# Attention's source alphas by staged one-hot products in pass 2, in place of gathers on POOL

## The chip, the cores and the metric

One core of a Trainium2 chip runs the whole program in one launch. The metric is the device time in microseconds (us): before the change 4203.94 us, the median of 10 runs that lie between 4200.74 and 4207.65 us.

A core has a matrix engine (PE; its weight loads are listed apart as PEld), VectorE (DVE), ScalarE (ACT), GpSimd (POOL), a queue engine (SP) that here only issues transfers, and 16 DMA engines. SBUF is the working memory with 128 lanes, PSUM holds what PE puts out, and DRAM holds the tables.

## The reference, cut to what matters

There are 12500 nodes of 256 features and 200000 edges (src, dst), sorted by dst. The first part is a graph convolution block with a residual; the second is an attention block that uses only the first n = 12500 edges.

```python
def gcn_conv(x, W, b):            # src, dst with one self loop per node added
    h = x @ W
    norm = dinv[src] * dinv[dst]
    return segment_sum(h[src] * norm[:, None], dst, n) + b

h = relu(layernorm(x))
h = h @ W_pre + b_pre
h = relu(gcn_conv(h, W1, b1)); h = relu(gcn_conv(h, W2, b2))
x = x + (h @ W_post + b_post)

h = relu(layernorm(x))
xt = (h @ weight).reshape(n, 4, 64)
alpha_l = sum(xt[src] * attn_l, -1)      # one number for each edge and head
alpha_r = sum(xt[dst] * attn_r, -1)
alpha = softmax(leaky_relu(alpha_l + alpha_r, 0.01), over the 4 heads)
tmp = sum over heads of alpha[:n, h] * xt[dst[:n], h]
out = x + the 64 columns of tmp, repeated 4 times
```

Row i of the attention's result belongs to edge i. Its dst is one of the first nodes, since edges are sorted by dst; its src is any node. So alpha_l of a row may need any node of the graph, the last one too.

## The kernel before, in words

**Tiles.** A tile is 128 edges, a chunk J = 14 tiles (1792 edges). There are 112 chunks, and NT = 98 windows of 128 nodes. The attention's 12500 edges are the first AC = 7 chunks, 98 tiles. Each attention chunk touches at most 128 nodes as dst, all within the first XW = 9 windows.

**The two passes.** `convolve` runs once for each convolution. For each tile POOL issues an indirect DMA that gathers 128 rows of the table by src (L1179, into fgot, four chunk buffers), and PE multiplies them by a one-hot of the edges' dst (L1187, into facc). VectorE builds a chunk's one-hots in one instruction (fhot, L1073; its node numbers are kept in PSUM as iota_p). When a chunk is done, ACT copies its sums (L1103), PE transposes them (L1038), and VectorE adds them into a sliding buffer (L1120). When the last edge of a window has been added, the window's own steps run: they are closures in a list, each with a number of tiles after which it is due, so that the instructions of a window's end stand between the products of later tiles. The instructions of each engine are in the order in which this list emits them.

**A window's end in pass 2** (`finish2`): the matrix W2 (d, L1269), bias and relu, W_post (f, L1285), the sum with the residual and its storing as kept_x (g), layernorm statistics, relu (h), transposes (i), a copy (k, ht, L1315), and the product with wg (q, L1324), which has 256 columns of xt, 4 of alpha_r and 4 of alpha_l. Step r (L1332) lets ACT copy the result and issue transfers: the alpha_l columns to the DRAM tables table_l and table_e, and for the first XW windows xt and alpha_r to table_r. The last LW = 3 windows don't write to table_e. Step names such as "fpx" in the list say which PSUM tile a step fills; a step that fills one waits in the list until it is read.

**Rows by dst.** For chunk c of the attention, `own_rows(c)` (L1374) is one gather on POOL of 128 consecutive rows of table_r; chunk 0 in window FROM = 40, the other six after pass 2. `turn_hots` (L1369) builds a one-hot of the edges' dst on VectorE. The rows of a tile are then one product of the two; those of the first 14 tiles are made during windows 40 to 53 (L1350, kept in `early`), the others in the last stage.

**The last stage, called the tail below.** The 98 tiles are handled in 15 groups: 13 of seven tiles, one of four and one of three. For each group:

- `keep` (L1418): SP loads kept_x. `ends_of` (L1446, L1448): PE makes the seven tiles' rows (256 columns of xt[dst] and 4 of alpha_r) through two PSUM buffers (fends), and ACT copies them to fxg in SBUF.
- `mix`: POOL gathers alpha_l by src, one indirect DMA for a tile (fal, L1456): 84 of table_l and, for the first 14 tiles, of table_e. What table_e lacks is added for these from three one-hots (hot_l, built at the start of pass 2, L1390) by `missing` (L1427).
- VectorE makes the softmax (L1460 to L1472, the exponential on ACT), scales the four heads (near and far, L1479), adds them (some L1482, more L1484, fmix L1486) and adds kept_x (fres, L1488). SP stores the group (L1494, L1497).

`keep` and `ends_of` of a group stand two groups ahead of its `mix`. Only SP and ACT issue direct transfers here; the gathers go through POOL's queue.

## Time and profile before

The profiled execution took 4204.65 us, of which the span from the first to the last instruction is 4202.8 us. The mean granted clock of PE is 0.797 of full speed.

| stretch (us from the start) | length | PE | DVE | ACT | POOL | granted clock | GB/s |
|---|---|---|---|---|---|---|---|
| start, 0 to 127 | 127.0 | 72.1 | 89.0 | 68.7 | 41.1 | 0.72 | 221 |
| pass 1, 127 to 2083 | 1956.0 | 1538.7 | 367.0 | 114.1 | 1477.7 | 0.78 | 121 |
| pass 2, 2083 to 4057 | 1974.0 | 1417.5 | 534.0 | 241.4 | 1486.9 | 0.83 | 130 |
| tail, 4057 to 4202.8 | 145.8 | 79.8 | 108.4 | 35.0 | 94.9 | 0.68 | 210 |

The engines' columns are busy us. A busy share under 100% doesn't mean that an engine has slack: POOL's time between two gathers is the issue of the next one, which the profile doesn't count as busy. Lines of the groups read "line, engine, operation, out<-in, count | busy us, mean ns of one | idle us before, and what ended it".

### The profile page before, as it was taken

Reading aid. Unit: us, or ns where it says so; the run is one execution under the profiler, and the core shown is the slowest. Engines: PE = TensorE matmul, PEld = TensorE weight load, DVE = VectorE, ACT = ScalarE, POOL = GpSimd, SP = SyncE. Lnnn points to the kernel's source line nnn. Section 1 sums busy time; section 2 is a strip of 40 time slices with the busy share of each in tenths; the row PEclk is TensorE's granted clock in tenths of the full one; section 3 lists DMA queues with packets and bytes.
Section 4 is the critical chain, followed back from the end, with each engine's and each line's share of the span. In section 5 each row is a group of like instructions: output and inputs, shape, how many; then the busy total and the mean of one; then the engine's idle time right before and its main releaser. Section 6 shows DMA issues by size and latency. Waiting matters only on the chain. (4 is left out here: it accounts for less than half of the span.)

```text
span 4202.8 us, 31693 instructions
## 1 busy us (share of the span) xinstructions
PE 3108.1 (74%) x10423; PEld 1960.2 (47%) x10423; DVE 1098.5 (26%) x2260; ACT 459.3 (11%) x1155; POOL 3100.5 (74%) x3346
## 2 busy tenths in 40 slices
PE   6487787787878788877667777777777777777774
PEld 5254444444444444444355545554455545455552
DVE  7321111111111111111132222222222222222238
ACT  5100000000000000000001111111111111111122
POOL 3677777777777777777777777777777777777766
PEclk7678878777777877788888888888888888877886
DMA  6544444444444444444445545554454445444556
GB/s 214 160 121 119 118 122 122 118 119 122 120 121 117 122 121 121 119 121 121 129 137 140 130 128 128 132 128 127 128 132 127 128 127 132 128 127 127 132 162 202
DMA packets 326197, 551.36 MB, mean 131 GB/s; under 512 B 96041, under 2 KB 224520, under 8 KB 326024
## 3 DMA queue, kind: packets, MB, share of 16 engines
q0 software_dynamic: 153520, 414.27, 37.3%
q1 hardware_dynamic: 126966, 118.80, 9.4%
q10 hardware_dynamic: 45538, 16.17, 1.5%
q8 instruction: 86, 1.41, 0.1%
q14 instruction: 87, 0.71, 0.1%
HBM read 495.73 MB, written 53.19 MB: 131 GB/s over the span
## 5 line engine op out<-in xcount | busy, mean ns | idle before, releaser
L1179 POOL DMA_INDIRECT fgot<-ftable,fsrc_t x3112 | 2944.7, 946 | 957.1 <-issue 898.0
L1187 PE MATMUL facc<-fgot,fhot 128*128 128x257 f32 (+1 forms) x6252 | 2368.4, 498 | 912.2 <-DMA fgot<-ftable,fsrc_t 870.5
L1187 PEld LDWEIGHTS facc<-fgot,fhot 128*128 128x128 f32 x6252 | 1265.8, 233 | 1856.6 <-DMA fgot<-ftable,fsrc_t 1410.7
L1120 DVE TENSOR_TENSOR buf<-buf,fturn 128x256 f32 x224 | 94.5, 422 | 1730.4 <-PE fturn L1038 1364.3
L1073 DVE TENSOR_TENSOR fhot<-iota_p,to_t 128x1792 f32<-128x1792 f32 x224 | 448.6, 2004 | 4.4 <-PE fpt L1094 4.4
L1276 DVE SCALAR_TENSOR_TENSOR fy<-rb,fb2c,fpz 128x128 f32<-128x128 f32 x194 | 58.8, 345 | 736.1 <-PE fpz L1269 735.1
L1103 ACT ACTIVATE fsums<-facc 128x257 f32<-128x257 f32 (+1 forms) x224 | 86.2, 385 | 1248.3 <-PE facc L1187 1242.4
L1290 DVE SCALAR_TENSOR_TENSOR fx<-fpo,fdinv,fxb 128x256 f32<-128x256 f32 x97 | 46.9, 484 | 477.5 <-PE fpo L1285 477.5
L1220 PE MATMUL fpo<-wf,buf 128*128 128x256 f32 x388 | 158.0, 552 | 0.4 <-DVE buf L1120 0.4
L1225 ACT ACTIVATE fo<-fpo,fdinv 128x256 f32<-128x256 f32 x97 | 46.0, 474 | 784.6 <-PE fpo L1221 784.6
L1220 PEld LDWEIGHTS fpo<-wf,buf 128*128 128x128 f32 x388 | 114.5, 296 | 29.6 <-DVE buf L1120 0.7
L1269 PE MATMUL fpz<-buf,fwb 128*128 128x128 f32 x776 | 123.8, 312 | 0.0
L1269 PEld LDWEIGHTS fpz<-buf,fwb 128*128 128x128 f32 x776 | 121.4, 235 | 2.3 <-DVE fy L1276 0.3
L1038 PE MATMUL fturn<-fident,self 128*128 128x128 f32 x396 | 84.0, 297 | 40.0 <-DMA self<-ftable 36.3
L1285 PE MATMUL fpo<-fwo,fz 128*128 128x256 f32 x388 | 112.3, 414 | 0.3 <-ACT fz L1279 0.3
L1456 POOL DMA_INDIRECT fal<-table_l,fsrc_t x84 | 81.2, 967 | 25.6 <-issue 23.2
L1038 PE MATMUL fturn<-fident,fsums 128*128 128x128 f32 x448 | 96.1, 300 | 0.5 <-ACT fsums L1103 0.5
L1446 PE MATMUL fends<-rows,hot_t 128*128 128x260 f32 x168 | 67.1, 566 | 35.9 <-ACT fxg L1448 35.4
L1315 ACT ACTIVATE ht<-fpt 128x256 f32<-128x256 f32 x97 | 37.2, 384 | 473.2 <-PE fpt L1311 473.2
L1038 PEld LDWEIGHTS fturn<-fident,fsums 128*128 128x128 f32 x448 | 70.5, 158 | 31.4 <-issue 8.4
L1221 PE MATMUL fpo<-bb,fins 2*128 2x256 f32 x194 | 85.1, 524 | 0.0
L1149 DVE COPY buf<-fturn 128x256 f32<-128x256 f32 x190 | 78.1, 411 | 0.0
(225 smaller groups left out, 1533.7 us busy)
## 6 DMA issues: line engine op xcount, KB each, us to landing
fgot<-ftable,fsrc_t POOLq DMA_INDIRECT x3112, 2.8
ftable<-fxt SPq DMA_DIRECT2D x14, 910.0 KB
self<-ftable SPq DMA_DIRECT2D x99, 128.0 KB
self<-ftable SPq DMA_DIRECT2D x97, 130.0 KB
ftable<-fo ACTq DMA_DIRECT2D x98, 128.0 KB
kept_x<-fx SPq DMA_DIRECT2D x98, 128.0 KB
fxb<-in_x_dram SPq DMA_DIRECT2D x97, 128.0 KB
fxt<-in_x_dram SPq DMA_DIRECT2D x13, 896.0 KB
```

The lines of the kernel that those rows point to most:

```text
L1038: nc.tensor.transpose(v["pt"][:, i * KC + k, :], rows[:, k * P:(k + 1) * P], ident)
L1073: nc.vector.tensor_tensor(h, iota_p[:, None, :].to_broadcast([P, n, P]), to[:, :, None].to_broadcast([P, n, P]), ALU.is_equal)
L1103: nc.scalar.activation(sb, acc, AF.Copy)
L1120: nc.vector.tensor_add(b, b, v["pt"][:, :KC, :])
L1149: nc.vector.tensor_copy(nxt[:, :, new], v["pt"][:, KC:, :])
L1179: nc.gpsimd.indirect_dma_start(out=got, out_offset=None, in_=table[:(NT - TW) * P, :] if some else table[:], in_offset=bass.IndirectOffset ...
L1187: nc.tensor.matmul(acc, hots[c][:, j, :], got[:, :width], start=(j == 0), stop=(j == nj[c] - 1 and not some))
L1220: nc.tensor.matmul(po, buf[:, k, :P], wf[:, k, :], start=(k == 0), stop=False)
L1221: nc.tensor.matmul(po, fs, bb, start=False, stop=True)
L1269: nc.tensor.matmul(pz[:, m, :], wb[:, k, m * P:(m + 1) * P], buf[:, k, :P], start=(k == 0), stop=(k == KC - 1))
L1285: nc.tensor.matmul(po, v["z"][:, m, :], wo[:, m, :], start=(m == 0), stop=(m == KC - 1))
L1456: nc.gpsimd.indirect_dma_start(out=al[:, i, :], out_offset=None, in_=(table_l if c else table_e)[:], in_offset=bass.IndirectOffsetOnAxis(a ...
```

## The change

The alpha_l of an edge is no longer fetched by a gather. A src is split into its low 7 bits and its window (src >> 7). The alpha_l columns of all windows stay in SBUF (`l_all`, 128 lanes by 98 windows by 4 heads). For a tile of edges, one product of a one-hot of the low bits with the columns of several windows gives, for each edge, the value at its lane in each of these windows; a mask "window equals src >> 7", a product and a sum pick the one that counts (`add_picked`), which is added to `al`.

This runs in five stages over windows 0 to 18, 18 to 36, 36 to 54, 54 to 72 and 72 to 84, each as soon as its windows are there. A part (`product` and `taken`) covers seven tiles, that is 70 parts of seven products of 72 columns (48 in the last stage); parts are appended to the steps of pass 2's windows, one to a window and two from window 73 on. Seven further parts first make alpha_r of all tiles, with 14 products of 4 columns each, and put it into `al`. Windows 84 to 97 (56 columns) follow in the tail (`late_al`). The one-hots of low bits are built one at a time, in two buffers, during pass 2 (`next_hot`: 44 in all), from a row that SP broadcasts to all lanes (`load_lo`).

`own_rows` becomes seven direct loads on SP in window 11, each with a register load of its first row. The writes to table_l and table_e go, and so do hot_l, `lates` and `missing`.

The tail is ordered anew: the softmax is made for a batch of four groups, heads 0 and 1 are scaled by ACT in pieces of 64 columns (`shared`), heads 2 and 3 by VectorE as before, fmix is in SBUF, and the sum with kept_x is made by POOL. Rows by dst are made up to six groups ahead (`fxg` has six buffers).

The other `own_rows`, `turn_late`, `keep` and out transfers keep their content and change place. The diff, cut:

```diff
-    table_l = dram.tile([NT * P, H], F32, name="table_l")
-    LW = 3
-    table_e = dram.tile([NT * P, H], F32, name="table_e")
+    lo_rows = dram.tile([NT, P], BF16, name="lo_rows")
+    STAGES = [(0, 18), (18, 36), (36, 54), (54, 72), (72, 84)]
+    LATE = STAGES[-1][1]
+    NL_W = NT - LATE
...
+    def split_sources(work):
...
+        lo = work.tile([NT, P], BF16, name="lo_b", bufs=1)
+        nc.vector.tensor_copy(lo, r)
+        nc.sync.dma_start(lo_rows, lo)
+        h = work.tile([P, NT], I32, name="hi_i", bufs=1)
+        nc.vector.tensor_scalar(h, src_t[:, :AC, :].rearrange("p c j -> p (c j)"),
+                                P.bit_length() - 1, None, op0=ALU.arith_shift_right)
+        nc.vector.tensor_copy(hi_t, h)
...
+    l_all = ap.tile([P, NT, H], F32, name="l_all", bufs=1)
+    al = ap.tile([P, NT, H], F32, name="al_all", bufs=1)
...
         def r():
...
-            nc.scalar.activation(xa[:, d0:], v["px"], AF.Copy)
-            nc.scalar.dma_start(table_l[w * P:(w + 1) * P, :], xa[:, DR:])
-            if w < NT - LW:
-                nc.scalar.dma_start(table_e[w * P:(w + 1) * P, :], xa[:, DR:])
             if w < XW:
-                nc.scalar.dma_start(table_r[w * P:(w + 1) * P, :], xa[:, :DR])
+                xa = work.tile([P, DR], F32, name="fxa", bufs=1)
+                nc.scalar.activation(xa, v["px"][:, :DR], AF.Copy)
+                nc.scalar.dma_start(table_r[w * P:(w + 1) * P, :], xa)
+            nc.scalar.activation(l_all[:, w, :], v["px"][:, DR - d0:], AF.Copy)
...
+        o = steps[-1][0] + 2
+        if w == XW + 2:
+            steps.append((o, own_rows, None))
+            steps.append((o + 2, next_hot, None))
+        for _ in range(0 if w < XW + 4 else 1 if w < STAGES[-2][1] + 1 else 2):
+            if todo and todo[0][0] <= w:
+                _, product, taken = todo.pop(0)
+                steps += [(o, lambda f=product: f(psum), "fpx"), (o + 2, lambda f=taken: f(work), None)]
+                o += 4
         return steps
...
-    def own_rows(c):
-        nc.gpsimd.indirect_dma_start(
-            out=rows[c], out_offset=None, in_=table_r[:],
-            in_offset=bass.IndirectOffsetOnAxis(ap=row_i[:, c:c + 1], axis=0))
+    def own_rows():
+        for c in range(AC):
+            at = nc.values_load(base_i[0:1, c:c + 1], engines=(mybir.EngineType.SP,), min_val=0,
+                                max_val=(XW - 1) * P,
+                                skip_runtime_bounds_check_because="clamped on the chip")
+            nc.sync.dma_start(rows[c], table_r[bass.ds(at, P), :])
...
+    def load_lo(pool, c, bufs):
+        lo = pool.tile([P, CE], BF16, name="lo_all", bufs=bufs)
+        nc.sync.dma_start(lo, lo_rows[c * J:(c + 1) * J, :].rearrange("t p -> (t p)")
+                          .partition_broadcast(P))
+        return lo
+    def next_hot():
+        if not coming:
+            return
+        key, row = coming.pop(0)
+        hot = hot_of[key] = ap.tile([P, CE], F32, name="hot_s", bufs=2)
+        s, c = key
+        nc.vector.scalar_tensor_tensor(hot, row[0], base_b[:, c:c + 1] if s == "ends" else 0.0,
+                                       in_banks["lane"].to_broadcast([P, CE]),
+                                       op0=ALU.subtract, op1=ALU.is_equal)
+        if coming:
+            coming[0][1].append(coming[0][1].pop()())
+    def stage_parts(work):
+        def ends_part(c):
+            z = {}
+            def product(psum):
+                z["p"] = psum.tile([P, 512], F32, name="fpx", bufs=1)[:, :J * H]
+                z["p"] = z["p"].rearrange("p (t h) -> p t h", h=H)
+                for j in range(J):
+                    nc.tensor.matmul(z["p"][:, j, :], hot_of["ends", c][:, j * P:(j + 1) * P],
+                                     rows[c][:, D:], start=True, stop=True)
+            def taken(work):
+                nc.scalar.activation(al[:, c * J:(c + 1) * J, :], z["p"], AF.Copy)
+                next_hot()
+            return XW + 4, product, taken
+        def al_part(s, c, b):
+            w0, w1 = STAGES[s]
+            nw, t0, z = w1 - w0, c * J + b * G, {}
+            def product(psum):
+                z["p"] = psum.tile([P, 512], F32, name="fpx", bufs=1)[:, :G * nw * H]
+                z["p"] = z["p"].rearrange("p (t w h) -> p t w h", t=G, h=H)
+                for i in range(G):
+                    j = b * G + i
+                    nc.tensor.matmul(z["p"][:, i, :, :], hot_of[s, c][:, j * P:(j + 1) * P],
+                                     l_all[:, w0:w1, :], start=True, stop=True)
+            def taken(work):
+                add_picked(work, z["p"], w0, w1, t0, in_banks["iota"])
+                if b == 0 or (s, c) == (len(STAGES) - 1, AC - 1):
+                    next_hot()
+            return w1 + 1, product, taken
+        todo.extend(ends_part(c) for c in range(AC))
+        todo.extend(al_part(s, c, b) for s in range(len(STAGES)) for c in range(AC)
+                    for b in range(J // G))
+        for s in ["ends"] + list(range(len(STAGES))) + ["late"]:
+            for c in range(AC if s != "late" else 2):
+                coming.append(((s, c), [(lambda c=c: load_ends(work, c, 1)) if s == "ends" else
+                                        (lambda c=c: load_lo(work, c, 1))]))
...
+    def add_picked(pool, z, w0, w1, t0, iota):
+        n, nw = z.shape[1], w1 - w0
+        mask = pool.tile([P, G, max(b - a for a, b in STAGES)], F32, name="fmask", bufs=1)
+        mask = mask[:, :n, :nw]
+        nc.vector.tensor_tensor(mask, iota[:, None, w0:w1].to_broadcast([P, n, nw]),
+                                hi_t[:, t0:t0 + n, None].to_broadcast([P, n, nw]), ALU.is_equal)
+        nc.vector.tensor_tensor(z, z, mask[:, :, :, None].to_broadcast([P, n, nw, H]), ALU.mult)
+        some = pool.tile([P, G, H], F32, name="fsome", bufs=1)[:, :n, :]
+        nc.vector.tensor_reduce(some, z.rearrange("p t w h -> p t h w"), AX.X, ALU.add)
+        o = al[:, t0:t0 + n, :]
+        nc.vector.tensor_add(o, o, some)
...
+        stage_parts(work)
...
+        def turn_lo(c):
+            if c in los:
+                hot_a[c] = mp.tile([P, CE], F32, name="hot_a", bufs=2)
+                nc.vector.tensor_scalar(hot_a[c], los[c], lane, None, op0=ALU.is_equal)
...
-        def missing(g):
...
+            xa = ends[g] = mp.tile([P, G, D], F32, name="fxg", bufs=6)
             for i in range(n):
                 c, j = divmod(t0 + i, J)
...
-                px = psum.tile([P, DR], F32, name="fends", bufs=2)
-                nc.tensor.matmul(px, hot_t[c][:, j * P:(j + 1) * P], rows[c], start=True,
+                px = psum.tile([P, D], F32, name="fends", bufs=2)
+                nc.tensor.matmul(px, hot_t[c][:, j * P:(j + 1) * P], rows[c][:, :D], start=True,
                                  stop=True)
                 nc.scalar.activation(xa[:, i, :], px, AF.Copy)
...
-            al = mp.tile([P, G, H], F32, name="fal", bufs=4)
+        def late_al(g):
+            t0, n = groups[g]
+            z = psum.tile([P, G * NL_W * H], F32, name="flate", bufs=2)[:, :n * NL_W * H]
+            z = z.rearrange("p (t w h) -> p t w h", t=n, h=H)
             for i in range(n):
                 c, j = divmod(t0 + i, J)
-                nc.gpsimd.indirect_dma_start(
-                    out=al[:, i, :], out_offset=None, in_=(table_l if c else table_e)[:],
-                    in_offset=bass.IndirectOffsetOnAxis(ap=src_t[:, c, j:j + 1], axis=0))
-            s = mp.tile([P, G, H], F32, name="fs")[:, :n, :]
-            nc.vector.tensor_add(s, al[:, :n, :], xa[:, :, D:])
-            if t0 < J:
-                nc.vector.tensor_add(s, s, missing(g))
+                nc.tensor.matmul(z[:, i, :, :], hot_a[c][:, j * P:(j + 1) * P],
+                                 l_all[:, LATE:, :], start=True, stop=True)
+            add_picked(mp, z, LATE, NT, t0, iota_w)
...
+        def softmax(b):
+            t0 = groups[batches[b][0]][0]
+            n = min(4 * G, NT - t0)
+            s = al[:, t0:t0 + n, :]
...
+            nc.vector.tensor_mul(s, s, m[:, :, None].to_broadcast([P, n, H]))
+        h2 = H // 2
+        def shared(g):
+            (t0, n), xa = groups[g], ends[g]
+            near = shares[g] = mp.tile([P, h2, G, C], F32, name="near", bufs=2)
+            for i in range(n):
+                for h in range(h2):
+                    nc.scalar.activation(near[:, h, i, :], xa[:, i, h * C:(h + 1) * C], AF.Copy,
+                                         scale=al[:, t0 + i, h:h + 1])
+        def mix(g):
+            (t0, n), xa, xr = groups[g], ends.pop(g)[:, :groups[g][1], :], kept.pop(g)
+            near, xr = shares.pop(g)[:, :, :n, :], xr[:, :n, :]
+            share = psum.tile([P, G, h2], F32, name="share", bufs=1)[:, :n, :]
+            nc.vector.tensor_copy(share, al[:, t0:t0 + n, h2:])
             far = psum.tile([P, h2, 512], F32, name="far", bufs=1)
...
-            for v, o in ((near, 0), (far, h2)):
-                nc.vector.tensor_mul(v.rearrange("p h g c -> p g h c"), xh[:, :, o:o + h2, :],
-                                     share[:, :, o:o + h2, None].to_broadcast([P, n, h2, C]))
+            nc.vector.tensor_mul(far.rearrange("p h g c -> p g h c"),
+                                 xa[:, :, h2 * C:].rearrange("p g (h c) -> p g h c", h=h2),
+                                 share[:, :, :, None].to_broadcast([P, n, h2, C]))
             some = mp.tile([P, G, C], F32, name="some")[:, :n, :]
...
-            mixed = psum.tile([P, G, C], F32, name="fmix", bufs=1)[:, :n, :]
+            mixed = mp.tile([P, G, C], F32, name="fmix")[:, :n, :]
             nc.vector.tensor_add(mixed, some, more)
             res = mp.tile([P, G, D], F32, name="fres", bufs=2)[:, :n, :]
-            nc.vector.tensor_add(res.rearrange("p g (h c) -> p g h c", h=H),
-                                 xr.rearrange("p g (h c) -> p g h c", h=H),
-                                 mixed[:, :, None, :].to_broadcast([P, n, H, C]))
+            nc.gpsimd.tensor_tensor(res.rearrange("p g (h c) -> p g h c", h=H),
+                                    xr.rearrange("p g (h c) -> p g h c", h=H),
+                                    mixed[:, :, None, :].to_broadcast([P, n, H, C]), ALU.add)
...
+        NG1 = len(groups)
+        for g in range(3):
+            keep(g)
+        for g in range(4):
+            late_al(g)
+            ends_of(g)
+        softmax(0)
+        for c in range(2, 4):
+            turn_late(c)
+            turn_lo(c)
+        for g in range(4, 8):
+            ends_of(g)
+        shared(0)
+        for g in range(NG1):
+            if g + 1 < NG1:
+                shared(g + 1) if g + 1 not in [b[0] for b in batches] else None
+            mix(g)
+            if g + 3 < NG1:
+                keep(g + 3)
+            if g + 4 < NG1:
+                late_al(g + 4)
+                if g % 2:
+                    turn_lo(g // 2 + 4)
+            for b in range(1, len(batches)):
+                if g + 1 == batches[b][0]:
+                    softmax(b)
+                    shared(g + 1)
+            if g >= 2 and g + 6 < NG1:
+                if g % 2 == 0:
+                    turn_late(g // 2 + 3)
+                ends_of(g + 6)
```

## The prediction

> **What bounds the kernel now.** I read the page first (busy shares, groups), then a table of stretches over the end of pass 2 and the tail, then the chain, and last the lines of single instructions.
>
> ```profile
> PE 3108.1 (74%) x10423; PEld 1960.2 (47%) x10423; DVE 1098.5 (26%) x2260; ACT 459.3 (11%) x1155; POOL 3100.5 (74%) x3346
> L1179 POOL DMA_INDIRECT fgot<-ftable,fsrc_t x3112 | 2944.7, 946 | 957.1 <-issue 898.0
> L1456 POOL DMA_INDIRECT fal<-table_l,fsrc_t x84 | 81.2, 967 | 25.6 <-issue 23.2
> ```
>
> A gather costs POOL 0.946 us and 0.30 us of issue, 1.25 us in all. 3112 of them are 3890 us: POOL sets the pace of both passes. In the tail 98 more (84 from table_l, 14 from table_e) are 122.5 us.
>
> The stretches (length, busy us of PE, PEld, DVE, ACT, POOL, clock, DMA share, GB/s):
>
> ```profile
> 2200.00:4000.00 1800.00, 1306.71 (x4915) 923.03 (x4914) 476.32 (x1016) 222.87 (x592) 1361.36 (x1441) 0.82 0.50 129
> 4100.00:4120.00 20.00, 11.90 (x33) 6.85 (x32) 18.37 (x33) 5.89 (x18) 15.13 (x17) 0.82 0.72 234
> 4120.00:4140.00 20.00, 13.99 (x36) 8.45 (x36) 18.35 (x33) 7.24 (x22) 15.43 (x16) 0.69 0.76 234
> 4140.00:4160.00 20.00, 12.69 (x36) 7.12 (x34) 18.61 (x31) 6.27 (x19) 15.12 (x17) 0.80 0.73 230
> ```
>
> The chain (start, us, what) goes through the tail's gathers, but these rows show a second bound beside them: VectorE is busy 18.4 of 20 us. A group of seven tiles takes it 7.8 us, against 8.75 us of gathers. So taking the gathers away frees at most the difference; the rest comes only if VectorE's and the other queues' work per group shrinks.
>
> ```profile
> 4057.16 1.37 DMA table_l<-fxl
> 4058.53 0.93 POOL fal L1456
> ...
> 4158.34 2.27 DMA fal<-table_l,fsrc_t
> ...
> 4194.86 0.95 DVE fres L1488
> ```
>
> The first alpha of the last window leaves ACT at 4057.98, the last sum ends at 4195.81, and 7.0 us later its output has landed: the tail is 145 us of the span.
>
> **Pass 2, part by part.** POOL loses one own-row gather in window 40: -1.25 us. The other six (4041 to 4048) lay beside the last windows: 0.
> PE gets 98 + 490 products of 4 and 72 columns, each two instructions. Rows: 42 instructions with 4 columns took 5.85 and 6.70 us, 776 with 128 columns 123.8 us, so 0.14 to 0.16 us each, 0.3 per product, 176 us in all. Cover: PE's wait for gathers, 493.6 us in 2200 to 4000, 5.3 us a window. One part (7 products, 2.1 us) fits; two a window (4.2 us, windows 73 to 79 and 85 to 91) just fit, and four chunk buffers let POOL run 56 gathers, 70 us, ahead. So 0; without the cover up to 176.
> VectorE gets 44 one-hots (2.02 us, the fhot row's size) and 70 picks: mask 0.22, product and reduction of 504 values 0.65 each (448 take 0.62), sum 0.18, 1.7 us. 208 us on an engine 26% busy: 0.
> SP gets seven register loads with row loads in window 11 and 44 broadcast loads, 23 MB over some 1550 us (15 GB/s onto 129); behind them wait only the next window's rows, asked for a window (19 us) ahead. ACT loses two DMA issues a window. Both 0.
> One price remains on POOL: the short sum of a pick has both operands in SBUF. At 4143.53 such a one-hot from SBUF to SBUF (1.20 us) stretched the gather under it from 0.94 to 1.44 us, 40% of its length. 70 sums of 0.18 us then cost 0 to 12.6 us, by that row 5; three hot_l of the pass start go, -1.4. Pass 2 together: +2 (bounds -3 to +10).
>
> **The tail.** The order on the queues decides, which I walk through from 4056.7 (4057.98 less 1.25).
> To the first result. PE: late products of groups 0 to 3 (28 at 0.27 us, between the two rows above) and end rows of groups 2 to 7, 42 tiles. A tile cost 0.61 us (4.25 for seven, 4153.94) to 0.84 (5.88, 4058.03, clock 0.5); PE now runs without a gap, and in 2135 to 2156 such a run was at clock 1.00, so 0.62: 26 us. With masks and waits PE is through at 4093.4. ACT copies these end rows in order, and only behind them stands the scaling of group 0, 14 pieces. A piece of 64 by rows: copies of 4 and 256 columns take 0.174 and 0.384, so 0.22; a per-lane scale adds 0.09 (fo 0.474 against ht 0.384); neighbours overlap by 0.1: 0.2 to 0.25, I take 0.225, 3.2 us. VectorE adds its last 1.9 us: group 0 ends at 4098.9. Before, group 0 was out at 4081.5: 17.4 us behind, with VectorE idle from 4081.
> Groups 1 to 3. VectorE per group: share, far, some, more, mix 3.2 us (rows 1.09, 0.62, 0.62, 0.63), pick 0.2 + 0.57 + 0.57 + 0.2 for 392 values, a one-hot of 1.2 in two of three. That is 5.6. But the output sum now runs on POOL, right where VectorE's pick begins, and this trace shows what two such instructions do to each other:
>
> ```profile
> 10.19 2.80 DVE L634 TENSOR_TENSOR near_f<-fdst_r,low 112x1792 f32<-112x1792 int32 x1
> ...
> 9.98 1.13 POOL L622 TENSOR_SCALAR_AFFINE_SELECT sel<-sel 32x1024 f32<-32x1024 f32 x1
> 11.18 2.77 POOL L624 TENSOR_SCALAR_AFFINE_SELECT sel<-sel 32x1024 f32<-32x1024 f32 x1
> ```
>
> POOL's first select ends at 11.11; VectorE's two-operand sum, issued at 10.19, takes 0.9 us more than its 1.9 and ends when 11.1 + 1.9 is over; the second select, alone 1.08, waits for that until 12.99. One stands still while the other works. So the pick's last sum waits for POOL's output sum. POOL's price for 1792 values from two operands is in no row: below it lies the one-operand select's rate (1.08 us for 1024), 1.9 us; above it that rate for each operand, 3.8. The short two-operand rows (14 values 0.209, 42 values 0.254, 1.6 ns a value) give 3.1; I take 3.4, as short rows hide a rate. The group is then mix 3.2 + mask 0.2 + POOL 3.4 + sum 0.2 + 0.8 of one-hots = 7.8, as before: group 3 ends at 4122.2.
> Groups 4 to 7. A softmax batch and the scaling behind it open the stretch (13.6 us for group 4); after it PE's seven end rows 4.4, late products 1.9 and ACT's 3.2 in between make 9.1 to 9.6 a group; POOL hides under them. Group 7: 4163.0. Group 8, after a softmax, 4175.4. Groups 9 to 11, without end rows, 7.0 each: 4196.3. Last softmax (its subtraction waits for POOL) and scaling, 10.1; the two short groups 2.2 and 1.7: 4210.3. POOL, one sum and one landed output behind, ends at 4216.3; 7.0 us as before: 4223.3. By DMA's sums the stretch would not bind (some 32 MB at the 335 GB/s seen at 4064 to 4078 is 96 us).
>
> **Two rules of the skill that speak against the change.** The Trainium skill, GPSIMD Engine Reference, section 3.1, has POOL's two-operand add about twice as slow as VectorE's, 4497 ns for 2048 values. By that an estimate of the output sum is 3.95 us and the end 4.7 us later than with 3.4. The Trainium skill, SBUF — State Buffer, section "SBUF: two separate sides", calls the port pair of both an exclusive lock for the whole instruction; the two rows at 10 us agree. Were it not so, the sum would end at 4206.8.
>
> **Sum.** Span 4223.3 + 2 in pass 2 = 4225; around it lie 1.85 us (4204.65 less 4202.8): 4227. The profiled run is 0.7 us above the median of 4203.94, so 4226.
>
> **Rivals.** (a) The two engines do not shut each other out here, or POOL's sum costs the lower bound. Groups 0 to 3 and 9 to 11 then take 5.6 and 4.3 us, no waits: end 4206.8 and 4210.8, with pass 2 and the frame 4210 to 4214; with PE at its full clock throughout 4 us less. For it: most tail operations of VectorE have one operand in PSUM. Against it: mask, sum and softmax have not.
> (b) Faster: the queues overlap so well that VectorE's own work alone sets the pace. 13 us to the first softmax, 74 us of its work (15 x 3.15, 11 x 1.55, softmax 6, one-hots 6), some 12 of waits and 10 to the landing: 4166, 37 us faster. It decides once ACT scales group 0 near 4080, not 4093; half of that effect, with (a) and full clock, is 4193. Against it: ACT's order puts 28 copies before the scaling, and PE cannot deliver 42 tiles under 0.45 us each (the dense run's pace).
> (c) Slower still: pass 2 stops hiding the products, since VectorE's picks and PE wait on each other through one PSUM tile (2 us for each of 70 parts, 140 us in all) and POOL runs out of its 70 us of lead: 4230 to 4300. Against it: 493 us of slack.
> (d) PE stays at clock 0.5 to 0.7 in the tail as now: end rows 0.84, end 4234.6 to 4238, the upper end of the forecast: 4242.
>
> **Chances.** Within 0.2% (8.4 us, about what a measurement of this kernel can tell) lies 4195.5 to 4212.3. Forecast with (d), 4213 to 4246: 0.57; (a), mostly inside the band: 0.20; (b), from 4166 to about 4198: 0.18; (c): 0.05. That gives slower 0.62, same 0.18, faster 0.20. The range 4193 to 4246 leaves out most of (b) and (c); the forecast's own is 4213 to 4246.
>
> **What would show it.** Right: the 40 slices unchanged up to the last; POOL's gathers still 1.25 us apart in pass 2; VectorE idle from about 4081 to 4097 behind ACT; POOL's output sum 3 to 4 us, and VectorE's short sum in the pick as long as what is left of it. Wrong: the first output sum before 4090 (b), short sums of 0.2 us throughout (a), or waits of the gathers on PE (c).

## The result and the profile after

The changed kernel takes 4235.73 us (median of 8 runs, 4230.76 to 4240.42), against 4206.22 us (28 runs) of the kernel before beside it: a ratio of 1.0073, with a 95% interval of 1.0064 to 1.0082. It is about 30 us slower; 4226 was forecast.

The profiled execution has a span of 4228.8 us, 5 us under the median once the 1.8 us around it are added. The lines of its page that answer to those shown before (engine sums, then groups):

```profile
PE 3228.2 (76%) x11711; PEld 2103.1 (50%) x11711; DVE 1288.1 (30%) x2552; ACT 507.8 (12%) x1356; POOL 3051.3 (72%) x3256
...
L1196 POOL DMA_INDIRECT fgot<-ftable,fsrc_t x3112 | 2942.7, 946 | 956.9 <-issue 899.8
...
L1448 PEld LDWEIGHTS fpx<-l_all,hot_s 128*128 128x128 f32 x980 | 147.3, 228 | 5.4
L1588 POOL TENSOR_TENSOR fres<-fxr,fmix 128x1792 f32<-128x1792 f32 (+2 forms) x15 | 55.7, 3714 | 129.4 <-DVE fmask L1472 61.5
L1448 PE MATMUL fpx<-l_all,hot_s 128*128 128x72 f32 (+1 forms) x980 | 143.1, 308 | 0.0
```

The gathers of the passes are what they were: 946 ns each, 900 us of issue. The 98 gathers of the tail are gone, and in their place POOL makes 15 output sums. The 490 stage products, two instructions each, keep PE busy for 143 us of pass 2, 0.29 us a product (0.3 was forecast), and POOL doesn't notice: from the first gather of pass 2 to the last one's end it takes 1957.3 us before and 1954.1 us after (1954.3 to 1960.0 in later profiles of kernels with the new alphas).

So the loss lies in the tail. Its cleanest measure is the stretch from the last copy of alpha_l (the last instruction of pass 2 on ACT) to the end of the span, since the passes end up to 13 us apart in two profiles of the changed kernel. Before, it is 144.8 us (4058.0 to 4202.8); after, 179.6 (4049.2 to 4228.8).

The table of stretches of the tail after (length, busy us of PE, PEld, DVE, ACT, POOL, clock, DMA share, GB/s):

```profile
4073.50:4091.50 18.00, 17.71 (x60) 9.83 (x61) 4.39 (x5) 10.55 (x28) 0.00 (x0) 0.91 0.41 153
4098.00:4118.00 20.00, 3.45 (x15) 3.33 (x16) 19.17 (x24) 7.20 (x30) 10.79 (x3) 0.50 0.70 217
4130.00:4170.00 40.00, 27.14 (x112) 19.79 (x112) 22.61 (x41) 22.99 (x82) 15.88 (x4) 0.77 0.55 169
```

Three regimes follow each other. From 4073.5 PE and ACT make end rows and VectorE idles. From 4098 VectorE is the one that is busy (19.17 of 20 us), but a good part of that is waiting. From 4130 no engine is busy for more than 70%: they wait for each other. ACT's rows (start, us, what, idle before) show the end of the first regime:

```profile
4090.17 0.84 ACT L1533 ACTIVATE fxg<-fends 128x256 f32<-128x256 f32 x2 [0.33 <-PE fends L1531]
4091.34 0.39 ACT L1533 ACTIVATE fxg<-fends 128x256 f32<-128x256 f32 x1 [0.33 <-PE fends L1531]
4091.62 6.78 ACT L1568 ACTIVATE near<-fxe,al_all 128x64 f32<-128x64 f32 x28
```

The 28th copy of end rows of groups 4 to 7 ends at 4091.7, and only then are heads 0 and 1 of groups 0 and 1 scaled. VectorE's rows, with its wait for that, and POOL's beside them:

```profile
4094.85 0.62 DVE L1582 TENSOR_TENSOR some<-near,far 128x448 f32<-128x448 f32 x1 [16.93 <-ACT near L1568]
...
4098.15 2.77 DVE L1478 TENSOR_TENSOR al_all<-al_all,fsome 128x28 f32<-128x28 f32 x1
...
4105.55 2.59 DVE L1478 TENSOR_TENSOR al_all<-al_all,fsome 128x28 f32<-128x28 f32 x1
...
4125.86 0.19 DVE L1478 TENSOR_TENSOR al_all<-al_all,fsome 128x28 f32<-128x28 f32 x1
...
4199.62 3.70 DVE L1554 TENSOR_TENSOR al_all<-al_all,fm 128x56 f32<-128x56 f32 x1
```

```profile
4096.90 3.98 POOL L1588 TENSOR_TENSOR fres<-fxr,fmix 128x1792 f32<-128x1792 f32 x1 [61.53 <-DVE fmask L1472]
4104.14 3.96 POOL L1588 TENSOR_TENSOR fres<-fxr,fmix 128x1792 f32<-128x1792 f32 x1 [3.26 <-DVE fmix L1586]
...
4218.63 1.80 POOL L1588 TENSOR_TENSOR fres<-fxr,fmix 128x768 f32<-128x768 f32 x1 [2.69 <-DMA out_dram<-fres]
```

The same short sum of 28 values takes 0.19 us at 4125.86, when POOL is at rest, and 2.77 and 2.59 us beside POOL's sums: 4098.15 + 2.77 is 4100.92, and POOL's sum ends at 4100.88; 4105.55 + 2.59 is 4108.14 against 4108.10. The last line of POOL's rows is the end of the tail: its last sum waits another 2.69 us for one of two fres buffers, whose output has to land.

### The profile page after: what moved, and what is told of

It is laid out like the page before. It is cut to its first block, busy times and chain, and to the rows that moved or that the text cites. A ratio compares the mean times of both kernels' runs of the same rounds, so it can differ in the third digit from the quotient of the medians.

```text
span 4228.8 us, 34731 instructions
## 1 busy us (share of the span) xinstructions
PE 3228.2 (76%) x11711; PEld 2103.1 (50%) x11711; DVE 1288.1 (30%) x2552; ACT 507.8 (12%) x1356; POOL 3051.3 (72%) x3256
## 5 line engine op out<-in xcount | busy, mean ns | idle before, releaser
L1204 PE MATMUL facc<-fgot,fhot 128*128 128x257 f32 (+1 forms) x6252 | 2328.9, 488 | 797.9 <-DMA fgot<-ftable,fsrc_t 763.5
L1204 PEld LDWEIGHTS facc<-fgot,fhot 128*128 128x128 f32 x6252 | 1225.9, 227 | 1721.9 <-DMA fgot<-ftable,fsrc_t 1381.2
L1448 PEld LDWEIGHTS fpx<-l_all,hot_s 128*128 128x128 f32 x980 | 147.3, 228 | 5.4
L1588 POOL TENSOR_TENSOR fres<-fxr,fmix 128x1792 f32<-128x1792 f32 (+2 forms) x15 | 55.7, 3714 | 129.4 <-DVE fmask L1472 61.5
L1448 PE MATMUL fpx<-l_all,hot_s 128*128 128x72 f32 (+1 forms) x980 | 143.1, 308 | 0.0
L1237 PEld LDWEIGHTS fpo<-wf,buf 128*128 128x128 f32 x388 | 113.5, 293 | 29.2 <-DVE buf L1137 0.7
L1531 PE MATMUL fends<-rows,hot_t 128*128 128x256 f32 x168 | 59.9, 504 | 43.3 <-DVE share L1575 22.9
L1474 DVE TENSOR_TENSOR fpx<-fpx,fmask 128x504 f32<-128x504 f32 (+1 forms) x70 | 46.0, 657 | 142.4 <-PE fpx L1448 141.2
```

The lines of the kernel that those rows point to most:

```text
L1204: nc.tensor.matmul(acc, hots[c][:, j, :], got[:, :width], start=(j == 0), stop=(j == nj[c] - 1 and not some))
L1237: nc.tensor.matmul(po, buf[:, k, :P], wf[:, k, :], start=(k == 0), stop=False)
L1448: nc.tensor.matmul(z["p"][:, i, :, :], hot_of[s, c][:, j * P:(j + 1) * P], l_all[:, w0:w1, :], start=True, stop=True)
L1531: nc.tensor.matmul(px, hot_t[c][:, j * P:(j + 1) * P], rows[c][:, :D], start=True, stop=True)
```

## The experiments

Theory: the tail is slow because (1) ACT's order holds up the first group, (2) VectorE's instructions with two operands in SBUF stand still while POOL's sum runs, and (3) what the new alphas add to the tail (late products and picks) is more than the removed gathers freed. Rivals: PE's end rows set the pace whatever the order; the stretched sums are contention with DMA; taking the gathers away wins and only the new tail loses.

The first four runs went to a chip on which the gathers of both passes had to wait, for a reason that the traces don't show, and the kernel before took 4952.03 us. Whole times can't resolve the tail there, so those runs are read by the stretch, one profile for each kernel. (Their whole times were 1.0029, 1.0004, 0.9978 and 0.9966 of the kernel before, in the order below; only the last interval, 0.9934 to 0.9998, leaves out 1.) That the stretch doesn't depend on the chip is shown by two kernels that ran on both: 158.9 and 159.4 us, 159.2 and 158.5 us. Differences under 1 us are not read.

**The sum back on VectorE.**

```diff
+            bank = psum.tile([P, 512], F32, name="share", bufs=1)
...
-            mixed = mp.tile([P, G, C], F32, name="fmix")[:, :n, :]
+            mixed = bank[:, 64:].rearrange("p (g c) -> p g c", c=C)[:, :n, :]
...
-            nc.gpsimd.tensor_tensor(res.rearrange("p g (h c) -> p g h c", h=H),
-                                    xr.rearrange("p g (h c) -> p g h c", h=H),
-                                    mixed[:, :, None, :].to_broadcast([P, n, H, C]), ALU.add)
+            nc.vector.tensor_add(res.rearrange("p g (h c) -> p g h c", h=H),
+                                 xr.rearrange("p g (h c) -> p g h c", h=H),
+                                 mixed[:, :, None, :].to_broadcast([P, n, H, C]))
```

> The sum with kept_x goes back from POOL to VectorE (2.02 us a group there, fmix in PSUM again); all else as changed. Theory, queue order and mutual exclusion: the pick's last sum falls from 2.6 to 3.1 us to 0.2, so VectorE's groups stay near 7 us, but the last softmax is 3.5 us shorter and POOL's late sums at the end go: span about 4219 (4215 to 4222), against 4228.8. Rival, PE and the late products set the pace of the tail and POOL's sum is hidden: no gain, 4226 to 4232. Rival, the stretched sums come from DMA traffic and not from POOL: they stay over 1 us, and the span is longer, 4235 to 4250.

The stretch is 172.0 us, 7.6 less, as the theory had it (7 to 14). All pick sums are back at 0.17 to 0.19 us with the same transfers running, so POOL and not DMA stretched them. VectorE now spends 2.02 us a group on the sum itself, which takes back a part of what is won.

**One operand in SBUF.**

```diff
+        bank = psum.tile([P, 512], F32, name="share", bufs=1)
+        iota_b = bank[:, 256:256 + NT]
+        in_banks["some"] = bank[:, 16:16 + G * H]
...
-            add_picked(mp, z, LATE, NT, t0, iota_w)
+            add_picked(mp, z, LATE, NT, t0, iota_b)
...
-            nc.vector.scalar_tensor_tensor(s, s, SLOPE, s, op0=ALU.mult, op1=ALU.max)
-            m = mp.tile([P, 4 * G], F32, name="fm")[:, :n]
+            lo = bank[:, 128:128 + n * H].rearrange("p (t h) -> p t h", h=H)
+            nc.vector.tensor_scalar(lo, s, SLOPE, None, op0=ALU.mult)
+            nc.vector.tensor_tensor(s, s, lo, ALU.max)
+            m = bank[:, 64:64 + n]
```

> POOL keeps the output sum; in the tail every instruction of VectorE that had two operands in SBUF (mask, the pick's last sum, the softmax's leaky relu, subtraction and product) gets one of them in PSUM. Theory, mutual exclusion of POOL and two-operand instructions: POOL's sums stay at 3.97 us, the pick's last sum takes 0.2 us beside them, groups 1 to 3 follow each other in 4.9 to 5.9 us instead of 7.2 to 8.4, groups 4 to 7 stay at PE's pace, and the span is 4211 to 4217. Rival, plain contention for SBUF: the short sums stay over 1 us or POOL's sums grow, and the span is within 5 us of 4228.8.

The stretch is 169.3 us, 10.3 less; 12 to 18 was expected. VectorE's and POOL's rows in this kernel:

```profile
4847.52 0.18 DVE L1481 TENSOR_TENSOR al_all<-al_all,share 128x28 f32<-128x28 f32 x1
...
4852.46 0.18 DVE L1481 TENSOR_TENSOR al_all<-al_all,share 128x28 f32<-128x28 f32 x1
4852.56 3.40 DVE L1508 TENSOR_SCALAR hot_a<-lo_all,lane 128x1792 f32<-128x1792 bf16 x1
```

```profile
4846.26 3.99 POOL L1598 TENSOR_TENSOR fres<-fxr,fmix 128x1792 f32<-128x1792 f32 x1 [103.67 <-DVE fmask L1472]
4851.05 3.96 POOL L1598 TENSOR_TENSOR fres<-fxr,fmix 128x1792 f32<-128x1792 f32 x1 [0.80 <-DVE fmix L1596]
```

With its second operand in PSUM the pick's sum takes 0.18 us in the middle of POOL's sum: the mutual exclusion is shown, since the sum is otherwise the same instruction on the same 28 values. Group 1 follows group 0 after 4.9 us instead of 7.4. But the wait has moved on: the one-hot that comes next, 1.15 us alone, now takes 3.40 us and ends at 4855.96, 0.95 us after POOL's sum. Its tensor operand, its column of lane numbers and its result are all in SBUF. Groups 2 and 3 therefore still take 8.2 us each.

The Trainium skill, SBUF — State Buffer, section "Who interferes with whom", has both: two SBUF inputs contend with a POOL instruction that reads SBUF, and `tensor_scalar` can enter a mode that uses the shared port. The runs agree with both (2.6 to 3.1 us for 0.19, 3.40 for 1.15), but whether it is the mode or the column that holds up the one-hot, no run here separates. The prediction had the first and let the one-hots go without a wait.

**The order alone**, run twice (the second time on a chip with ordinary passes).

```diff
-        for g in range(4, 8):
-            ends_of(g)
         shared(0)
+        ends_of(4)
         for g in range(NG1):
...
-            if g >= 2 and g + 6 < NG1:
-                if g % 2 == 0:
-                    turn_late(g // 2 + 3)
-                ends_of(g + 6)
+            if g + 5 < NG1:
+                if g % 2 and g >= 3:
+                    turn_late((g + 5) // 2)
+                ends_of(g + 5)
```

> Only the order of emission changes: the scaling of group 0 comes ahead of the end rows of group 4, and later end rows are made one group at a time between the scalings, five groups ahead instead of six. Theory, ACT's order holds up the first result: group 0's fmix ends near 4078 instead of 4096.7, VectorE's wait of 16.9 us goes, and about all of that is kept, since PE's remaining 57 us of work end near 4131: span 4208 to 4215. Rival, PE's end rows set the pace anyway: the gain of group 0 is lost again by group 7, span 4222 to 4229.

> The new order alone once more, on another chip than the one whose passes were 750 us longer. By the stretches (158.9 us from the last alpha_l to the end, against 179.0 and 179.6 of the changed kernel) the whole time is 20 us under the changed kernel's: 1.002 to 1.004 of the kernel before, if the passes take what they did. If the gain in the tail doesn't carry to the whole, 1.006 or more.

The stretch is 158.9 and 159.4 us, 20 to 21 less than the changed kernel's. Group 0's fmix ends 30.6 to 30.9 us after the last alpha_l instead of 47.5; these 17 us last to the end, where they are 20. The whole time is 1.0023 of the kernel before (1.0014 to 1.0032), against 1.0073. So the gain is not lost again to PE's end rows, and the rival falls.

**The new alphas with the tail of before**: softmax by group, all four heads and the output sum on VectorE, end rows two groups ahead, and a late product and pick for each group where the gathers were. Also run twice. The lines are against the kernel before.

```diff
+                late_al(g)
             if g >= 2:
                 mix(g - 2)
...
-            for i in range(n):
-                c, j = divmod(t0 + i, J)
-                nc.gpsimd.indirect_dma_start(
...
-            s = mp.tile([P, G, H], F32, name="fs")[:, :n, :]
-            nc.vector.tensor_add(s, al[:, :n, :], xa[:, :, D:])
+            s = al[:, t0:t0 + n, :]
```

> The new source alphas (stages in pass 2, late products and picks) with the tail of before otherwise: VectorE scales all four heads and makes the output sum, the softmax is made group by group, end rows two groups ahead. Theory, VectorE's work sets this tail: 9.5 us a group for 13.9 groups and ten one-hots of 1.2 us, 144 us from 4052, then 7 us to the landing: span 4200 to 4208, about the 4202.8 of before, so that the new alphas alone neither win nor lose and the loss lies in how the tail was ordered anew. Rival, the late products and picks themselves are what costs: span 4215 or more.

> The new alphas with the tail of before, once more. Its stretch was 159.2 us where the kernel before has 144.8; pass 2 ends at most 5 us earlier than before. So the new alphas alone should cost 9 to 14 us: 1.002 to 1.0035 of the kernel before. Rival, taking the gathers away wins elsewhere (the slow chip had it 0.3% faster than before): 0.999 or less.

The stretch is 159.2 and 158.5 us, 14 longer than before, and the whole time 1.0020 of it (1.0011 to 1.0029), 8.6 us slower. In this tail, a table of stretches has VectorE at 92%:

```profile
4076.00:4196.00 120.00, 70.82 (x293) 53.65 (x292) 110.70 (x204) 27.52 (x83) 0.00 (x0) 0.72 0.60 201
```

Groups now follow each other after 9.9 us on average (fmix of group 1 at 30.2 us, of group 12 at 139.4), against 8.4 before (33.2 and 125.6). The 98 gathers of 1.25 us are gone and nothing was freed, since VectorE stood right beside them; a pick of 1.6 us a group and five one-hots of low bits, 1.15 us each, come on top. The first of the two expectations, that the alphas neither win nor lose, was missed, though not by as much as its rival had it (12 us or more); the second was met. So the change loses in both of its halves: 14 us of the stretch by the alphas, 20 more by the new tail. On the first chip, whose gathers wait, the whole time of this kernel was 0.9966 of the kernel before: there something is won ahead of the tail that outweighs it, and what that is is not shown.

**The changed kernel once more**, as a control on the chip of the next runs.

> The changed kernel itself, unaltered, on the chip of these runs. The stretch from the last copy of alpha_l (the last instruction of pass 2 on ACT) to the end of the span took 179.6 us before on another chip; if this stretch doesn't depend on the chip, as the runs so far suggest, it is 178 to 182 us here, while the passes may differ by hundreds of us. If it does depend on it, the comparisons of stretches across chips fall.

179.0 us, and 1.0067 (1.005 to 1.0084) in the whole.

**Order and one operand together; order and sum on VectorE.**

> The new order of the end rows and the single SBUF operand together. Alone they shortened the stretch from the last alpha_l to the end by 20.7 and 10.3 us (from 179.6). If the two causes are independent, it is 147 to 150 us; if ACT and PE by turns set the pace in the new order (PE waits for two PSUM buffers while ACT scales), VectorE's gain is hidden in the middle groups and it is 151 to 156 us. One-hots that follow POOL's sum still wait for it: 3.4 us instead of 1.1.

> The new order with the output sum on VectorE, so that POOL does nothing in the tail. No mutual exclusion can be left: all pick sums at 0.2 us, all one-hots at 1.1. VectorE then has 6.9 us a group: 26 us to its first group, 13.9 groups, 11 us of one-hots, 6 of softmaxes, 7 to the landing, 146 us if VectorE sets the pace; with ACT and PE by turns at 8.3 us in the middle groups 150 to 156. Rival, only POOL off the path helps: under 140.

150.4 and 150.6 us; 0.9999 (0.9989 to 1.0008) and 1.0003 (0.9993 to 1.0012) of the kernel before. Of 31.0 us that the order and the single operand gave alone (20.7 and 10.3 from 179.6), 29.2 remain together: the two causes are nearly independent. The one-hots took 1.2 to 1.7 us and not 3.4, since in this order POOL's sum is nearly over when they start. POOL's sum beside one-operand instructions and VectorE's sum come to the same, so in this order the choice is free; what is left is set elsewhere.

**No late stage.** `late_al` makes neither products nor picks, so the alpha_l of windows 84 to 97 is left out of the sums.

> The changed kernel without the late stage: no products and no picks of windows 84 to 97 in the tail, so that their alpha_l is left out of the sums; all else as changed. If the late stage sets the tail together with the order (it delays PE's first end rows by 10 us, and its picks are what waits for POOL), group 0's fmix ends near 38 us after the last alpha_l instead of 47.5 and the groups after it follow every 4 to 8 us: the stretch is 138 to 150 us. Rival, order and output sum alone set it: 165 us or more.

143.4 us, and 0.9977 (0.9968 to 0.9987). Group 0's fmix ends at 36.8 us, and the next three groups follow after 3.4, 5.0 and 4.7. The late stage is thus 36 us of the changed kernel's tail, more than its own work on any engine (98 products in 31 us on PE, 15 picks of some 1.6 us on VectorE). PE's first end row starts 0.1 us after the last alpha_l instead of 8.7, and the pick's sums that wait for POOL are gone; the gain is 10.7 us at group 0, 11.0 more by group 3 and 14.5 behind it. How much of that is the delay and how much the waits, this run doesn't separate. The gains of order (20.7), one operand (10.3) and no late stage (36) overlap: their sum is more than the loss of 34.8.

**Pairs on ACT, and one-hots that read PSUM.** On top of order and one operand, two scaling pieces of a group follow each copy of an end row, the softmax of a batch comes a group earlier, the one-hots of chunks 4 and later take their lane numbers from PSUM, and the sums of the two short groups are VectorE's, the one of four tiles with a result buffer of its own.

```diff
+        def pair(ge, gs):
+            made = ends_of(ge) if ge < NG1 else iter(())
+            pieces = shared(gs) if gs < NG1 else iter(())
+            for _ in range(G):
+                next(made, None)
+                next(pieces, None)
...
-                nc.vector.tensor_scalar(hot_a[c], los[c], lane, None, op0=ALU.is_equal)
+                    nc.vector.scalar_tensor_tensor(hot_a[c], los[c], 0.0,
+                                                   lane_b.to_broadcast([P, CE]),
+                                                   op0=ALU.subtract, op1=ALU.is_equal)
...
+            (nc.vector if n < G else nc.gpsimd).tensor_tensor(
```

> The new order, with each end row's copy followed by two scaling pieces on ACT so that PE goes on meanwhile; POOL's sum with no two-operand instruction of VectorE beside it; the later one-hots read their lane numbers from PSUM (2.02 us each); the softmax ahead of the group before its batch; the sums of the two short groups on VectorE. Theory, the waits found so far are all there is: ACT's 6.1 us a group and VectorE's 5 to 7 set the pace, and the stretch from the last alpha_l to the end is 125 to 138 us, under the 144.8 of the kernel before; the one-hots stay near 2 us beside POOL's sums. Rival, one-hots wait for POOL in any form: they take over 3 us and the stretch is 140 to 150.

137.5 us, under the 144.8 before, and the whole kernel is faster than before: 4194.47 against 4206.39 us, 0.9969 (0.9959 to 0.998). Five things change at once here, so their shares are not known apart. The one-hots don't wait in this form (another instruction, `scalar_tensor_tensor`, with the lane numbers in PSUM); VectorE's row, and POOL's sum that covers it:

```profile
4103.62 2.07 DVE L1505 SCALAR_TENSOR_TENSOR hot_t<-to_all,base_b,share 128x1792 f32<-128x1792 int32 x1
```

```profile
4102.11 3.97 POOL L1619 TENSOR_TENSOR fres<-fxr,fmix 128x1792 f32<-128x1792 f32 x1 [4.16 <-DVE fmix L1614]
```

The one-hot ends at 4105.69, before POOL's sum does (4106.08), and its 2.07 us are what this form takes without a sum beside it (2.0 to 2.1 us in the 44 of pass 2).

**Two tiles in a PSUM buffer.** One copy of 512 columns for two tiles of end rows, four tiles ahead instead of two.

```diff
-                px = psum.tile([P, D], F32, name="fends", bufs=2)
+            for i in range(0, n, 2):
+                m = min(2, n - i)
+                px = psum.tile([P, 2, D], F32, name="fends", bufs=2)
...
+                nc.scalar.activation(xa[:, i:i + m, :], px[:, :m, :], AF.Copy)
```

> The paired kernel, with two tiles of end rows in each of the two PSUM buffers and one copy of 512 columns for both: four tiles ahead instead of two, 44 copies instead of 84. In the paired kernel PE and ACT still wait for each other at every tile. Theory, that is what the middle groups cost now: the stretch falls from 137.5 us to 127 to 134. Rival, VectorE's picks and one-hots bind there already: 136 to 139.

132.4 us, and 0.9956 (0.9943 to 0.997): the best kernel of this study, 16 us under the one before. It lies in the expected 127 to 134, so the rival, that VectorE's picks and one-hots bind there already, falls; whether the deeper buffer or the fewer copies helped is not separated. Its chain (start, us, what) ends in transfers:

```profile
4162.15 3.99 POOL fres L1621
4166.16 7.74 DMA out_dram<-fres
...
4174.02 3.98 POOL fres L1621
4178.02 0.38 SPq L1628
...
4178.44 5.86 DMA fxr<-kept_x
```

POOL's sum of group 11 (4174.02) waits for a buffer whose output, group 9's, takes 7.74 us to land, and the last load of kept_x stands on SP behind an output. More buffers for fres and fxr come next; they weren't tried.

## Why the prediction was right, and where it was off

The sign, the place and the causes (ACT's order, the exclusion, picks that cost more than the gathers freed) were right, and 4235.7 lies in the range of 4193 to 4246. The closeness of the whole is in part luck, as the sum at the end of this list shows. Step by step:

- **What bounds the kernel.** Right: that VectorE stands beside the gathers is what the alphas with the old tail show (9.9 us a group after 8.4).
- **Pass 2.** +2 us (−3 to +10) was said; it is a small gain. (The cover was read a little too large: in 2200 to 4000 PE waits 472 us for gathers; 493.6 belongs to 2150 to 4060.) In nine comparisons on chips with ordinary passes the whole time of a kernel with the new alphas is 2.4 to 7.4 us better, against the kernel before, than its stretch (the control 31.8 us slower with a stretch 34.2 longer, the alphas alone 8.6 with 13.7), so 2 to 7 us are won ahead of the tail. In the first profile after, POOL's gathers run ahead of those before in two steps, 1.7 us at the start of pass 2, where hot_l is no longer built, and 1.3 at window 40 (own_rows). The 5 us for picks under gathers are 0: all 70 short sums take 0.19 to 0.26 us, 58 of them beside a gather, and no gather after 2101 us takes more than 1.0 us. The row that priced them was a one-hot, and all five one-hots of the tail before have a gather of 1.4 us beside them; a short sum has none. That was the wrong row.
- **To the first result.** 42.2 us after the last alpha_l was said (4098.9 less 4056.7), 47.5 it is. PE's rows (two instructions are one product):

```profile
4049.23 8.86 PE L1542 MATMUL flate<-l_all,hot_s 128*128 128x56 f32 x42 [0.26 <-ACT l_all L1351]
4057.88 5.95 PE L1531 MATMUL fends<-rows,hot_t 128*128 128x256 f32 x14
4063.66 1.66 PE L1542 MATMUL flate<-l_all,hot_s 128*128 128x56 f32 x14
4065.16 4.17 PE L1531 MATMUL fends<-rows,hot_t 128*128 128x256 f32 x14
4073.61 17.69 PE L1531 MATMUL fends<-rows,hot_t 128*128 128x256 f32 x56 [4.27 <-DVE hot_t L1389]
```

"PE now runs without a gap" failed: PE waits 4.3 us, 4069.3 to 4073.6, for a one-hot that VectorE builds only after the softmax, whose exponential waits on ACT behind the copies and a table load of 1.28 us. The full clock failed too: the first 21 late products took 0.42 us each and not 0.27, and the first seven end rows 0.85 and not 0.62, at a granted clock of 0.54 from 4049 to 4058 and 0.56 from there to 4064. The other seven products (0.24) were faster than said, the other 35 end rows (0.60 and 0.63) as said.
- **Groups 1 to 3.** 7.8 us each was said, 7.4, 8.4 and 8.4 it is. POOL's sum takes 3.97 us, not the 3.4 that I took between rows; the row of short sums, at 1.6 ns a value, hid a rate of 2.2. The estimate of 3.95 by the figure in the Trainium skill, GPSIMD Engine Reference, section 3.1, was right.
- **Groups 4 to 14.** Group 3 to 7 in 42.4 us (40.8 said), 7 to 8 in 13.3 (12.4), 8 to 11 in 22.7 (20.9), 11 to 14 in 14.9 (14.0). Three whole sets of seven end rows took 5.3 to 6.0 us, at granted clocks of 0.53 to 0.71, not 4.4. The last softmax's subtraction does wait for POOL, 3.70 us.
- **The end.** 14.7 us from the last mix instead of 13.0: the 2.69 us wait for an fres buffer was not in the sum.

These are 13 us of stretch in all (166.6 said, 179.6 measured), the first result alone 5.3 of them. The gather of window 40 was taken off twice, in the start of the walk at 4056.7 and in the +2 for pass 2, another 1.25 us. Against that, pass 2 won some 5 us where a loss of 2 was said. So misses of 14 and of 7 us stand against each other; with a kernel before that itself took 2.3 us more beside the new one (4206.22 for 4203.94), the whole came out 10 us over the forecast.

**The rivals.** (a), no exclusion or a cheap sum, is refuted by sums of 2.6 to 3.1 us. (b), the queues overlap, did not happen in this order, but the case was real: with its condition met, group 0's fmix at 31 to 33 us instead of 47.5, and fewer waits behind it, the best kernel stands at 4195.15 (beside 4210.98 for the kernel before); the condition alone, in the new order, left it at 4221.19. Its 74 us of VectorE's work are 76 by its own terms. (c) is refuted by POOL's 1.25 us a gather. (d), the clock stays low, came about halfway: 28 end rows ran at a clock of 0.91 (0.63 us each), the first seven and three later sets of seven at 0.53 to 0.71, and all 84 took 0.71 us on average, between the 0.62 of the forecast and the 0.84 of (d). Its end of 4234.6 to 4238 is a stretch of 178 to 181 us, and 179.6 was measured; but the wait for the one-hot, the 3.97 us sum and the buffer at the end, none of them in (d), are part of that.

## What to carry to other kernels

Before work is taken off the engine that paces a stretch, read the busy share of the next one there: here 18.4 of 20 us said that 122 us of gathers could free a tenth of that at most, and the replacement's pick cost more than this tenth. Before a sum is moved to POOL, look at what VectorE runs beside it: here sums with two operands in SBUF and one-hots from SBUF to SBUF stood still, while the sums with one operand in PSUM, and one-hots in the slower form (2.0 us for 1.15) with a column in PSUM, ran through. And on an engine that works in order, look at what stands ahead of the first piece that others wait for: 28 copies ahead of one scaling, and the order of the rows behind them, were 20 us of this kernel, two thirds of its loss.

## What the runs showed that I had not expected

The exclusion works both ways. In the kernel without the late stage one-hots come first and POOL's sums stand still: five of thirteen full sums take 4.5 to 4.9 us instead of 3.97. Two sums at the start of its tail, and the one-hot between them:

```profile
4086.99 8.76 POOL L1581 TENSOR_TENSOR fres<-fxr,fmix 128x1792 f32<-128x1792 f32 x2 [50.91 <-DVE share L1568]
```

```profile
4090.03 1.89 DVE L1505 TENSOR_SCALAR hot_a<-lo_all,lane 128x1792 f32<-128x1792 bf16 x1
```

The one-hot waits for the first sum (3.98 us, to 4090.97) and ends at 4091.92. The second sum, which had started beside it, ends at 4095.75, 3.8 us later, nearly the length of a whole sum: it stood still meanwhile.

The chip of the first four runs is the other surprise: the same programs had passes some 750 us longer there, with POOL waiting between its gathers, while the tail was the same to within 1 us. Its cause is open.
